# Attention block with feed-forward: weight sums, weight mixing, a copy and two norm stages moved in the hand-written order

## Chip, cores and metric

The kernel runs on one core of a Trainium2 chip. The metric is the device time of one execution in microseconds; the time of a kernel is the median of its runs. In the listings PE is TensorE, PEld its weight load, DVE VectorE, ACT ScalarE, POOL GpSimd and SP SyncE, which issues the DMAs. A letter L and a number name a line of the kernel.

## What is computed

One layer on 8 sequences of 1024 tokens, width 512, 16 heads of 32, inner width 2048, all fp32. Both sublayers are sandwiched between norms:

```
qvk = layernorm(x) @ Wqvk                      # q, v, k: 16 heads of 32
scores = einsum('bshi,bthi->bsth', q, k) + causal mask;  scores = scores / sqrt(512)
weights = softmax(scores, axis=2)
wv = einsum('bsth,bthi->bshi', weights, v)
x = x + layernorm(wv @ Wo)
hidden = layernorm(x) @ W1 + b1
imag   = w_imag * sin(theta + hidden * 0.1)
q      = hidden + (cos(theta) * w_real + sin(theta) * w_imag) * imag * 0.1
x = x + layernorm(relu(q) @ W2 + b2)
```

## The kernel before

**Batches and stages.** A loop runs over the 8 sequences, here called batches 0 to 7. For each, `attention` goes over four groups of four heads. Per group, `find_maxima` makes the scores in four runs and reduces each row to its maximum (matmuls L675; VectorE L693 and L705; exponentials and row sums for the first half, ACT L725). The maxima are split into three bf16 parts on GpSimd (L653, L660, L662) and transposed on TensorE (L114). Then `weigh` makes the scores again, transposed, with the maxima subtracted by a matmul (L781, L792), takes the exponentials (ACT L807) and masks the diagonal squares (GpSimd L811). `weighted_values` multiplies with v (L830) into an accumulator bank.

**Sums and division.** For the second half of the queries the weights of a group are added up on VectorE (`add_weights`, L859) and summed over keys by four-head matmuls with ones (`weight_sums`, L845). `divide` takes ACT Ln (L864) and Exp (L866) of the sum, and VectorE multiplies the accumulator (L867) into `wvT`. For the first half, the sums come into the exponentials through the maxima, and the accumulator is copied to `wvT` by ACT (L960). The last steps of a group are kept in `late` and `summing` and run inside the next group's `find_maxima`: after its first run, `sums()` is called.

**Fillers.** Between the runs of `find_maxima` generators fill TensorE: `advance(work, fill)` projects q, k and v of the next group (L513, L522, L530, with copies L538 on ACT and additions L565, L566 on GpSimd). The list `MAX_FILL` gives how many steps after each run. In the last group of batch 7 there is nothing left to project.

**After attention.** `finish_block` runs per half: projection (`project`, L1013), copy out (L1022), norm, addition to x, norm, transposition (L114) and mixing for the fast products (L1051). Half 0 runs inside attention's last group, half 1, `between`, inside the feed-forward.

**Feed-forward.** `feed_forward` has 8 steps of first-layer products and a ninth in which only second-layer products are left, numbered s = 0 to 8. Both layers use a scheme of seven products in place of eight. `hidden(s)` makes the first layer's products "1", "6", "2", "7", "5", "4", "3" (L1127) and combines them on VectorE (L1197) and ACT (L1210) into `hid`. `wave_in` (VectorE L1148, L1153, L1154, ACT sine L1155) and `wave_out` (VectorE L1170, L1176) apply the transform; `wave_out` of a step comes in the next one, but in step 7 in the same. `blocks` on GpSimd (L1243, four operations each) makes the mixed inputs hm of the second layer, whose products (L1262) follow in four quarters. A quarter is drained by ACT L1314 and VectorE L1274 into two tiles yb and then passes through `end`: bias on GpSimd (L1343), moments (VectorE L309, L310), rstd (GpSimd L316, L317), normalisation (L328), addition to x (L1352), store to HBM (L1356) and reload of x for the next batch (L121). `end` is a staged generator: stage by stage for the two tiles, advanced by `advance_ends(1)` in the loop of the feed-forward. `measure_ahead` takes moments of a later batch's input (xin, loaded at L391) in steps 7 and 8.

```
            (1, 2, 1, 3),
            (7,) * 6,
        )
        BETWEEN = ((0, 1, 2), (2, 3), (1, 3))
        MEASURE = {STEPS - 1: 2, STEPS: 7}
```

The first lines are the last two rows of `SECOND`: how many second-layer products follow each place of steps 7 and 8. `BETWEEN[s]` names the places of step s at which half 1 of `finish_block` goes on.

**Weights.** In batch 0 `mix_weights` prepares the mixed weights of both layers once: it loads parts (w_t), makes sums on GpSimd (L288) and stores all to scratch in HBM (L302). It is a generator of 34 pieces, advanced by `mixing` in the deferred steps of attention. Later, SP loads the mixed weights tile by tile (wm, L1103) into a ring of 18 buffers.

**Order.** Within each engine the order is that in which the kernel issues (`in_order`, `keep_in_program_order`); an engine takes its queue from the front. All eight PSUM banks of 2 KB per partition are given out in turn by `psum`, and `drained` marks the instruction after which a bank is free.

Of the kernel before, what the change touches and what calls it, by code (L numbers as in the profile page):

```python
# [32 lines left out]
def kernel(  # L33
# [14 lines left out]
    nc = tc.nc  # L48
# [61 lines left out]
    def in_order(instruction):  # L110
        tc.keep_in_program_order(instruction)
# [257 lines left out]
    def advance(work, steps=1):  # L369
        for _ in range(steps):  # L370
            if next(work, None) is None:
                return

    def finish(work):
        for _ in work:
            pass
# [120 lines left out]
    def project_qkv(b, g):  # L497
# [122 lines left out]
    MAX_RUNS = (  # L620
        (((0, 0), (2, 0)),),
        (((5, 0),), ((3, 0),)),
        (((4, 0),), ((1, 0), (5, 1))),
        (((6, 0),), ((4, 1), (6, 1))),
    )
# [10 lines left out]
    def find_maxima(b, g, work, sums, more):  # L636
# [84 lines left out]
        def exponentials(left):  # L721
            for es, cols, mx, row in left:
                for m in range(2):
                    in_order(
                        nc.scalar.activation(  # L725
                            es[:, m, cols],
                            es[:, m, cols],
                            AF.Exp,
                            bias=mx[:, m : m + 1],
                            scale=-1.0,  # L730
                            accum_out=row[:, m : m + 1],
                        )
                    )

        left = []
        for n, (run, fill) in enumerate(zip(MAX_RUNS, MAX_FILL[g > 0])):
            new = [x for pieces in run for x in run_unit(pieces)]
            if n == 0:
                sums()
            exponentials(left)  # L740
            left = new
            if n == len(MAX_RUNS) - 1:
                split(0)
            advance(work, fill)
            if n >= len(MAX_RUNS) - 2:
                advance(more)
        mT = transpose_maxima(parts_q[0], nc.scalar.copy)
# [10 lines left out]
    def transpose_maxima(parts, evacuate):  # L758
        pt = psum([P, TPB, P], BF16)
        for n in range(TPB):  # L760
            transpose_on_pe(pt[:, n, :], parts[:, n, :], ident_h)
        mT = small.tile([P, HALF], BF16, tag="mT", name="mT", bufs=2)
        evacuate(mT, pt.rearrange("p n t -> p (n t)"))
        drained(pt)
        return mT
# [104 lines left out]
    def attention(b, wvT, after):  # L870

        late = []
        adding = []
        summing = [None]

        def sums():
            if summing[0] is not None:
                summing[0]()  # L880
                summing[0] = None

        def flush():
            while late:
                late.pop(0)()

        def projections(g):
            if g + 1 < NG:
                return project_qkv(b, g + 1)
            if g + 1 == NG and b + 1 < B:  # L890
                return project_qkv(b + 1, 0)
            return iter(())

        work = projections(0)
        for g in range(NG):
            more, first = after(g)
            early = more if first is None else iter(())
            mT, later = find_maxima(b, g, work, sums, early)
            if not b and g + 2 < NG:
                mix_weights_of_group(b, g + 2)  # L900
            mTs = [mT]
            at = 0
            for c in range(2):
                accs = []
                total = None
                units = KEY_UNITS[c]
                for u, keys in enumerate(units):
                    if at < 2:
                        later(at)
                    weights, placed = weigh(b, g, c, keys, mTs[c])  # L910
                    if at < 2:
                        advance(work)
                    if at == 2:
                        mTs.append(
                            transpose_maxima(
                                parts_q[1], lambda *a: in_order(nc.vector.tensor_copy(*a))
                            )
                        )
                    if c and u == 0:
                        finish(work)  # L920
                        work = projections(g + 1)
                        advance(work)
                    if c and u == len(units) - 2:
                        advance(work)
                    if first is None and (at < 2 or c and u >= len(units) - 2):
                        advance(more)
                    while len(late) > (g < NG - 1 and c and u > 0):
                        late.pop(0)()
                    while adding and (g == NG - 1 or not late or u > 1):
                        add_weights(*adding.pop(0))  # L930
                    apart = g == NG - 1 and u >= len(units) - 2
                    if c and u == 0:
                        total = weights, placed
                    elif c and not apart:
                        adding.append((total[0], weights, placed))

                    def step(accs=accs, u=u, last=u == len(units) - 1, weights=weights, c=c, g=g,
                             placed=placed, total=total, apart=c and apart, dst=wvT[c][:, g, :]):
                        if u == 0:
                            accs.append(psum([P, HALF]))  # L940
                        acc = accs[0]
                        weighted_values(acc, b, g, u == 0, last, weights, placed)
                        if apart:
                            if not last:
                                accs.append(psum([P, HALF]))
                                weight_sums(accs[1], *total, last=False)
                            weight_sums(accs[1], weights, placed, first=False, last=last)
                        if last and c:

                            def whole():  # L950
                                if apart:
                                    whole_sum = accs[1]
                                else:
                                    whole_sum = psum([P, HALF])
                                    weight_sums(whole_sum, *total)
                                divide(acc, whole_sum, dst)

                            summing[0] = whole
                        elif last:
                            nc.scalar.copy(dst, acc)  # L960
                            drained(acc)

                    late.append(step)
                    advance(mixing)
                    if first is not None and at >= first:
                        advance(more)
                    at += 1
            while adding:
                add_weights(*adding.pop(0))
            if g == NG - 1:  # L970
                flush()
                advance(more)
                sums()
            else:
                finish(more)

                def ended():
                    flush()
                    sums()

                summing[0] = ended
        return more

    def finish_block(b, half, wvT, x2T, mixed, out_w):
# [75 lines left out]
    def feed_forward(b, x2T, mixed, before, between):  # L1060
# [3 lines left out]
        STEPS = 2 * NSTEP  # L1064
# [10 lines left out]
            (1, 2, 1, 3),  # L1075
            (7,) * 6,
        )
        BETWEEN = ((0, 1, 2), (2, 3), (1, 3))
        MEASURE = {STEPS - 1: 2, STEPS: 7}
        hids = {}  # L1080
        ahead = []
# [280 lines left out]
        def advance_ends(steps):  # L1362
            for _ in range(steps):
                while quarters and next(quarters[0], None) is None:
                    quarters.pop(0)
# [8 lines left out]
        for s, quota in enumerate(SECOND):  # L1374
            if s == NSTEP:
                finish(between)
            products = hidden(s) if s < STEPS else iter(())
            for n, more in enumerate(quota):
                advance(products)
                if s in MEASURE and n >= len(quota) - MEASURE[s]:  # L1380
                    advance(measuring)
                if s < len(BETWEEN) and n in BETWEEN[s]:
                    advance(between)
                advance_ends(1)
                if (s, n) == (1, 1):
                    advance(units)
                advance(units, more)
                if s == STEPS and n == 3 and b + 1 < B:
                    fetch(b + 1, 1)
                if s == STEPS and n >= 2:  # L1390
                    advance(mixing_x)
# [6 lines left out]
    mixing = mix_weights()  # L1398
# [81 lines left out]
```

## Time and profile before

| | |
|---|---|
| time, median of 3 runs | 3686.82 us (3686.36 to 3687.15) |
| profiled execution | 3686.16 us |
| its span | 3684.4 us |
| mean granted TensorE clock | 0.995 |
| TensorE busy | 3587.1 us, 97% |
| VectorE busy | 2752.1 us, 75% |
| ACT busy | 1453.6 us, 39% |
| GpSimd busy | 1451.3 us, 39% |
| moved by DMA | 488.83 MB, mean 133 GB/s |

The profile is one execution. A group's busy time is the sum over its instructions; a wait is idle time of an engine ahead of an instruction, put down to the instruction that released it last. Times inside the span count from the first instruction. Batch 4 is used as the example of a steady batch: its maxima for group 3 begin near 2039 us, its feed-forward's step 7 near 2268 us.

### The profile page before, as it was taken

How to read it: one execution, taken by the hardware profiler on the slowest of the kernel's cores; microseconds unless marked ns; L12 is line 12 of the kernel's file. 1: busy time of each engine (PE TensorE's matmuls, PEld its weight loads, DVE VectorE, ACT ScalarE, POOL GpSimd, SP SyncE). 2: the span in 40 equal slices, each digit the busy share in tenths (PEclk: the TensorE clock that was granted, in tenths of full speed). 3: DMA queues.
4: the chain of work that ended last, by engine and by line, in shares of the span. 5: the costliest groups of instructions: out<-in, count | busy, mean ns of one | idle time of the engine just before them, and what ended most of it. 6: DMA issues, size and time to landing. Idle time of an engine off the chain costs nothing.

```text
span 3684.4 us, 61975 instructions
## 1 busy us (share of the span) xinstructions
PE 3587.1 (97%) x22561; PEld 2342.0 (64%) x22561; DVE 2752.1 (75%) x5587; ACT 1453.6 (39%) x2812; POOL 1451.3 (39%) x1984
## 2 busy tenths in 40 slices
PE   8899999999999999999999999999999999999998
PEld 4446874478644786447864488544885548854587
DVE  5867777677686787767867778776887768777686
ACT  4553126531365213652146521465115642156310
POOL 5543363233532345313453234542344323543243
PEclk9999999999999999999999999999999999999999
DMA  4433761047610475105751058410683116820166
GB/s 145 150 134 118 240 212 44 30 128 241 206 41 21 144 245 186 53 10 161 252 162 53 12 177 264 131 53 15 195 275 105 47 35 197 263 78 18 58 216 190
DMA packets 312001, 488.83 MB, mean 133 GB/s; under 512 B 29904, under 2 KB 91408, under 8 KB 311696
## 3 DMA queue, kind: packets, MB, share of 16 engines
q1 hardware_dynamic: 309536, 483.02, 41.5%
q8 instruction: 180, 2.95, 0.3%
q10 hardware_dynamic: 2160, 1.84, 0.2%
q14 instruction: 125, 1.02, 0.1%
HBM read 451.71 MB, written 33.03 MB: 132 GB/s over the span
## 4 chain that ended last, share of the span: by engine, by line
PE 78%; DVE 12%; issue 5%; ACT 2%; POOL 2%; DMA 0%; SPq 0%; DVEq 0%; POOLq 0%; ACTq 0%
PE banks L1127 16%; PE banks L1262 16%; PE banks L545 8%; PE banks L675 8%; PE banks L530 6%; PE banks L1013 6%; PE banks L830 5%; PE banks L792 5%; PE banks L513 3%; DVE w L859 3%; PE banks L114 2%; PE banks L781 2%; DVE u L1148 1%; PE banks L845 1%; DVE u L1154 1%
## 5 line engine op out<-in xcount | busy, mean ns | idle before, releaser
L807 ACT ACTIVATE w<-banks 128x1024 f32<-128x1024 f32 (+1 forms) x640 | 562.1, 938 | 286.0 <-PE banks L792 285.4
L859 DVE TENSOR_TENSOR w<-w 128x1024 f32<-128x1024 f32 (+3 forms) x416 | 427.2, 1080 | 136.3 <-PE banks L830 130.4
L811 POOL TENSOR_SCALAR_AFFINE_SELECT w<-w 128x256 f32<-128x256 f32 x512 | 293.2, 592 | 547.9 <-ACT w L807 482.7
L1127 PE MATMUL banks<-x2T,wm 128*128 128x256 f32 x2048 | 477.3, 381 | 22.9 <-DVE hid L1197 15.8
L705 DVE CUSTOM_DVE_ANT_0 es<-banks,mask 128x128 f32<-128x128 f32 (+3 forms) x1024 | 432.2, 484 | 62.4 <-PE banks L675 62.4
L1262 PE MATMUL banks<-wm,hm 128*128 128x256 f32 x2048 | 472.9, 381 | 2.4 <-POOL hm L1243 1.8
L1127 PEld LDWEIGHTS banks<-x2T,wm 128*128 128x128 f32 x2048 | 387.2, 190 | 86.0 <-DVE hid L1197 19.0
L1155 ACT ACTIVATE u<-u 128x1024 f32<-128x1024 f32 x128 | 135.4, 1058 | 774.6 <-DVE u L1154 765.7
L1262 PEld LDWEIGHTS banks<-wm,hm 128*128 128x128 f32 x2048 | 388.4, 191 | 60.2 <-POOL hm L1243 8.1
L693 DVE TENSOR_REDUCE mx<-banks 128x1 f32<-128x512 f32 (+1 forms) x384 | 309.6, 861 | 122.7 <-PE banks L675 122.5
L1262 PE MATMUL banks<-wm,hid 128*128 128x256 f32 x1536 | 359.8, 380 | 6.5 <-DVE yb L1274 6.5
L1243 POOL TENSOR_TENSOR hm<-hid 128x256 f32<-128x256 f32 x256 | 216.6, 846 | 367.4 <-DVE hid L1176 367.4
L675 PE MATMUL banks<-k,q 32*128 32x512 f32 (+3 forms) x3072 | 329.6, 515 | 0.4 <-DVE mx L705 0.2
L792 PE MATMUL banks<-q,k 32*128 32x512 f32 (+3 forms) x3072 | 324.3, 492 | 0.0
L1262 PEld LDWEIGHTS banks<-wm,hid 128*128 128x128 f32 x1536 | 289.9, 190 | 48.2 <-DVE yb L1274 9.7
L830 PE MATMUL banks<-w,v 128*32 128x512 f32 (+3 forms) x3072 | 312.4, 495 | 5.4 <-POOL w L811 3.3
L530 PEld LDWEIGHTS banks<-wqvk,xnT 128*128 128x128 f32 x2048 | 242.0, 193 | 73.6 <-issue 50.9
L725 ACT ACTIVATE es<-es,mx 128x512 f32<-128x512 f32 (+3 forms) x512 | 279.6, 550 | 1.9 <-DVE mx L705 1.9
L530 PE MATMUL banks<-wqvk,xnT 128*128 128x128 f32 x2048 | 268.6, 283 | 0.0
L675 PEld LDWEIGHTS banks<-k,q 32*128 32x128 f32 x3072 | 154.0, 185 | 146.6 <-DVE mx L705 66.9
L1127 PE MATMUL banks<-mix,wm 128*128 128x256 f32 x1024 | 241.9, 379 | 0.0
L1013 PE MATMUL banks<-wo,wvT 128*128 128x512 f32 x512 | 235.6, 600 | 3.2 <-DVE wvT L867 3.2
(135 smaller groups left out, 5115.0 us busy)
## 6 DMA issues: line engine op xcount, KB each, us to landing
wm<-w_mixed SPq DMA_DIRECT2D x1344, 256.0 KB, 2.9
xin<-in_L_attn_h_dram SPq DMA_DIRECT2D x112, 256.0 KB, 4.0
wqvk<-in_L_attn_Wqvk_dram SPq DMA_DIRECT2D x93, 256.0 KB, 5.6
out_dram<-x SPq DMA_DIRECT2D x64, 256.0 KB, 2.0
x<-in_L_attn_h_dram SPq DMA_DIRECT2D x60, 256.0 KB, 3.2
w_mixed<-w_t SPq DMA_DIRECT2D x56, 256.0 KB, 3.0
wmix<-qk_mixed SPq DMA_DIRECT2D x42, 256.0 KB, 5.0
wo<-in_L_attn_Wo_dram SPq DMA_DIRECT2D x32, 256.0 KB, 2.7
```

The costliest lines, as they stand in the source:

```text
L530: nc.tensor.matmul(pv[:, t - t0, :], xnT[b, t // TPB][:, kc, (t % TPB) * P : (t % TPB + 1) * P], w_of[b, g, 1][:, kc, :], start=(kc == 0), ...
L545: nc.tensor.matmul(pq, w[:, kc0 + kc, :], moving[:, kc, :], start=kc == 0, stop=kc == 1,)
L675: nc.tensor.matmul(scs[j // 2][:, j % 2, at : at + n], queries[r, i * P : (i + 1) * P], keys[r, k0 : k0 + n], start=True, stop=True,)
L693: nc.vector.tensor_reduce(out=mx[:, m], in_=sc[:, m, cols], op=ALU.min, axis=mybir.AxisListType.X,)
L705: nc.vector.tensor_tensor_reduce(out=es[:, m, cols], in0=sc[:, m, cols], in1=mask[:, HALF - n :], scale=1.0, scalar=FMAX, op0=ALU.add, op1 ...
L792: nc.tensor.matmul(sts[j // 2][:, j % 2, cols], all_keys[r, kb * P : (kb + 1) * P], all_queries[r, q0 : q0 + n], start=False, stop=True,)
L807: in_order(nc.scalar.activation(w[:, :, :width], st[:, :, :width], AF.Exp, scale=-1.0))
L830: nc.tensor.matmul(acc[r, HALF - n :], v[b, g][:, kb, r], weights[j // 2][:, j % 2, cols], start=first and k == 0, stop=last and k == len( ...
L859: in_order(nc.vector.tensor_add(t[:, :, q], t[:, :, q], w[:, :, cols]))
L1013: nc.tensor.matmul(y, wvT[:, kc, t * P : (t + 1) * P], out_w[kc], start=(kc == 0), stop=(kc == KC - 1),)
L1127: nc.tensor.matmul(bank[:, n, :], w[:, n, kc, :], moving[:, kc, :], start=first and kc == 0 and n == 0, stop=kc == 1 and n == 1, skip_grou ...
L1262: nc.tensor.matmul(region, a[:, n], w[:, n], start=start and n == 0, stop=last and n == 1, skip_group_check=True,)
```

## The change

In `find_maxima` a second call of `sums()` stands behind the first filler, and `advance(mixing, 3)` behind the fillers of the first three runs; the advance of `mixing` in `attention`'s deferred step is gone. `sums()` now clears `summing` before it calls what was stored, and what is stored between groups is `flush` alone: the first call runs the last deferred step, which stores the sums, and the second call runs those. So the ones matmuls and the division come after the filler. The copy of the first half's accumulator goes from ACT to VectorE. In the feed-forward, the third place at which half 1 of `finish_block` goes on in step 0 is 3 in place of 2, and in step 7 `advance_ends` is called only at the last place.

```diff
@@ find_maxima
             advance(work, fill)
+            if n == 0:
+                sums()
+            if n < len(MAX_RUNS) - 1:
+                advance(mixing, 3)
             if n >= len(MAX_RUNS) - 2:
                 advance(more)
@@ attention
         def sums():
             if summing[0] is not None:
-                summing[0]()
-                summing[0] = None
+                summed, summing[0] = summing[0], None
+                summed()
...
                         elif last:
-                            nc.scalar.copy(dst, acc)
+                            in_order(nc.vector.tensor_copy(dst, acc))
                             drained(acc)
 
                     late.append(step)
-                    advance(mixing)
...
                 finish(more)
-
-                def ended():
-                    flush()
-                    sums()
-
-                summing[0] = ended
+                summing[0] = flush
@@ feed_forward
-        BETWEEN = ((0, 1, 2), (2, 3), (1, 3))
+        BETWEEN = ((0, 1, 3), (2, 3), (1, 3))
...
                 if s < len(BETWEEN) and n in BETWEEN[s]:
                     advance(between)
-                advance_ends(1)
+                if s != STEPS - 1 or n == len(quota) - 1:
+                    advance_ends(1)
```

The instructions stay the same in number and size; the copies alone change their engine. On TensorE, 23 sets of ones matmuls come after the 16 filler matmuls of L530 instead of before them, and in each batch one projection (L1013) comes after the products "5" and "4" of step 0. In the changed kernel line numbers are 4 higher from `find_maxima` into `attention`, and 2 lower from `finish_block` on.

## Prediction

> **What bounds the kernel now.** I read the page's busy times first, then TensorE's waits, then the timelines around the places that the diff touches. The profiled execution took 3686.16 us, its span 3684.4 us, so 1.76 us lie around the span; the median of the three runs is 3686.82, 0.66 more.
>
> ```profile
> PE 3587.1 (97%) x22561; PEld 2342.0 (64%) x22561; DVE 2752.1 (75%) x5587; ACT 1453.6 (39%) x2812; POOL 1451.3 (39%) x1984
> ...
> PE 78%; DVE 12%; issue 5%; ACT 2%; POOL 2%; DMA 0%; SPq 0%; DVEq 0%; POOLq 0%; ACTq 0%
> ```
>
> TensorE is the bound. The change adds and removes no matmul, so it can only open or close gaps of TensorE. This is the list of them (waiting matmul and line, what it waited for, total us, times, longest):
>
> ```profile
> PE banks L1127 <- DVE hid L1197: 15.8, 8, 2.0
> PE banks L781 <- ACT w L807: 13.7, 33, 0.5
> ...
> PE banks L845 <- DVE w L859: 11.2, 4, 4.7
> PE banks L1127 <- DVE u L1197: 7.1, 8, 0.9
> ...
> PE banks L830 <- POOL w L811: 3.3, 5, 1.0
> ...
> PE banks L1262 <- POOL hm L1243: 1.8, 6, 0.3
> ```
>
> The line of 15.8 us is one gap of 1.96 us per batch, in feed-forward step 7; the 11.2 us lie in batch 0.
>
> **1. Ends held back in step 7 (8 batches).** The gain first. In batch 4 VectorE does this in step 7 (start, duration):
>
> ```profile
> 2281.61 0.94 DVE L328 TENSOR_SCALAR yb<-yb,mv,rs 128x512 f32<-128x512 f32 x1
> 2282.58 1.09 DVE L1352 TENSOR_TENSOR x<-x,yb 128x512 f32<-128x512 f32 x1
> 2283.60 0.68 DVE L1197 TENSOR_TENSOR hid<-banks,u 128x512 f32<-128x512 f32 x1
> ```
> ```profile
> 2281.35 1.03 PE L1262 MATMUL banks<-wm,hm 128*128 128x256 f32 x4
> 2284.34 0.70 PE L1127 MATMUL banks<-x2T,wm 128*128 128x256 f32 x2 [1.96 <-DVE hid L1197]
> ```
>
> Two normalisations (L328), two additions (L1352) and one moment (L309, L310) of the finished quarter stand ahead of the hidden addition that product "3" waits for. Taken away, that addition ends by about 2281.5, TensorE goes on at 2282.38, and 1.96 us are gained.
>
> The price is on GpSimd. The second tile's rstd (L316, L317) is issued with these stages, and GpSimd works in order. Before:
>
> ```profile
> 2277.67 0.22 POOL L316 TENSOR_SCALAR rs<-mv 128x1 f32<-128x1 f32 x1 [3.43 <-DVE mv L310]
> 2277.97 0.57 POOL L317 TENSOR_TENSOR rs<-rs,mhalf 128x1 f32<-128x1 f32 x1
> ...
> 2282.23 0.90 POOL L1243 TENSOR_TENSOR hm<-hid 128x256 f32<-128x256 f32 x1
> 2283.21 1.05 POOL L1243 TENSOR_TENSOR hm<-hm,hid 128x256 f32<-128x256 f32 x1
> ...
> 2296.26 0.73 POOL L1243 TENSOR_TENSOR hm<-hid 128x256 f32<-128x256 f32 x1 [10.62 <-DVE hid L1176]
> ```
>
> There are three blocks of four hm operations behind the first rstd: at 2278.51, 2282.23 and 2296.26. In the changed order the rstd moves behind the block of 2278.51 and still stands ahead of the block of 2282.23. Its input, the second tile's moment, moves on VectorE to behind both wave_out of step 7. So the block of 2282.23, whose inputs are ready early, now waits behind the rstd for a moment that comes some 15 us later. Who waits for that block? The second-layer products with hm at 2291.35:
>
> ```profile
> 2291.35 1.03 PE L1262 MATMUL banks<-wm,hm 128*128 128x256 f32 x4
> ```
>
> They now have 2291.35 - 2283.21 - 1.05 = 7.1 us of slack. When does the moment end after the change? The first hidden addition starts when its product is done, 2280.8, the second when the product with mixl ends, 2281.4, and ends at 2282.1. From there VectorE's own row: first wave 2.8 (the same four operations take that at 2289.01 to 2291.88), addition 0.6, second wave 2.9, i.e. to 2288.4; the two wave_out took 2291.80 to 2296.11, 4.3, so to 2292.7. Then, in the changed order, one xin moment (0.8), the first tile's L328 (0.54 without a neighbour on GpSimd), L1352 (0.69) and the second tile's moment (0.9): 2295.6. The rstd takes 0.85, and the first two hm operations 1.55 (0.73 each in the 2296.26 rows, with a gap of 0.08): 2298.05. TensorE, 1.96 us earlier than before, arrives at 2289.4 and stands for 8.7 us. Against before the products start 2298.05 - 2291.35 = 6.7 us late. The gap of 0.29 at the third hm block goes, as that block follows by 2301.5 and is wanted at 2304. Net +6.4 per batch. Batches 6 and 7 have no xin moment there: +5.6. Sum 6 x 6.4 + 2 x 5.6 = **+49.6 us** (44 to 62: the hidden additions 0.7 us sooner, or both waves at the slower durations that they have beside GpSimd).
>
> SyncE: the two stores and the reload of x also move behind that point, so some ten wm loads queue behind a store that waits for L1352 until about 2298.5. A weight is used 15 us after its load may be issued and lands in 2.9 us at the median, and TensorE itself is 6.7 us late: hidden; without that cover I would count 2 to 3 us a batch. The drains of this quarter (L1274) come up to 2 us late, but the next quarter uses the other banks, and nobody wants these for 12 us.
>
> **2. Sums behind the first filler (23 places).** The ones matmuls (L845), ACT's Ln and Exp (L864, L866) and VectorE's product (L867) now come after 16 filler matmuls (L530), 1.98 us later. The second run of the maxima needs the banks that they free. In batch 4, group 3: L845 goes from 2040.05 to 2042.03, so Ln starts at 2043.32 and L867 ends after 0.60 + 0.63 + 0.68 plus 0.1 of handing over, at 2045.35. The matmuls that take its bank stood at 2044.17: +1.2 us, seven times, as batch 7 has no filler there. In groups 1 and 2 the ones matmuls now wait inside for the last addition L859, 0.94 us that the filler would hide; L867 then ends 1.2 after the moment when the bank is wanted: net +0.3, sixteen times. Sum 8.4 + 4.8 = **+13 us**. Bounds: the 0.92 gained sixteen times with no bank late, -15; 1.2 at all 23, +28. I take the middle, because the trace already shows the next run's weight loads (L675) waiting for L867, 4.8 us in 21 places.
>
> **3. Mixing of weights in the maxima (batch 0).** Before, GpSimd's additions (L288) run among the weights' exponentials:
>
> ```profile
> L288 POOL TENSOR_TENSOR w_t<-w_t x32: 1255/1308/2258, 74.6 to 265.3; 128x512 f32<-128x512 f32 x32
> ```
>
> Minimum, median and maximum are 1255, 1308 and 2258 ns: beside VectorE's L859 they stretch, and so do L859 and the masks L811. The weigh phases of groups 0, 1, 2 take 32.9, 30.6 and 32.3 us in batch 0 against 23.6, 23.6 and 24.3 in batch 4: 9.3 + 7.0 + 8.0, with a transposition gap of 1.54 some 25.9 us lost. The measuring of batch 1 stays in group 1 and keeps about 3.5 of that: 22.4 come back. In the new place the additions stand in GpSimd's queue ahead of the parts of the maxima (L653, L660) that the transpositions (L114) wait for: seven to eight additions of 1.27 in place of an idle GpSimd make those late by 4, 2.4 and 3.7 us, 9 us together. Net **-13 us** (between -26, when the delay is hidden, and +10, when each addition waits for its load besides).
>
> The stretching has a rule in the Trainium skill (GPSIMD Engine Reference, Specifications): GpSimd's SBUF interfaces are shared with VectorE and contended by VectorE instructions with two SBUF inputs. By it alone the maxima, which read PSUM, would return all 25.9, and the sum would be 13 us lower; it says nothing on the queue.
>
> **4. Copy to VectorE (32 copies).** L960 takes 616 ns on ACT; the nearest VectorE row is L867, 680 ns from PSUM. VectorE idles there for some 6 us before L859, which waits for TensorE anyway, and ACT's next exponentials wait for TensorE's scores: **0**. Bounds: -13.7 if all waits for L807 went, +22 (32 x 0.68) if all lay on the path. I take 0, since the 0.5 us gaps lie at ACT's own chain of four exponentials of 0.94.
>
> Against this edit speaks the skill's page Advanced Engine Details and Errata, The Read-Write Bubble, which puts ScalarE closer to PSUM and VectorE closer to SBUF. By the two rows that is 0.06 us a copy, 2 us in all if none were hidden.
>
> **5. One projection later (BETWEEN).** The gap of 0.89 (L1127 <- u) is VectorE's backlog in step 0; its work there stays the same: **0** (-7 to +7). The moved norm also issues an rstd, but the hm block behind it waits for a later wave_out in either order.
>
> **Sum.** 49.6 + 13 - 13 = +50: 3684.4 + 50 + 1.76 = 3736.2 for the profiled execution, about **3737** for the median.
>
> **Rivals.**
> - *Faster:* the block of 2282.23 is not held, because the second tile's moment ends before 2289.4 less 2.4, that is by 2287. Then the gaps of 1.96 and 0.29 of part 1, 2.25 us, are won eight times: -18 + 13 - 13 gives 3669. Against it: the moment stands behind both wave_out on VectorE, and these alone ended at 2296.11. It decides for faster as soon as the stall is under 2 us. 0.06.
> - *Slower, but by half:* the hold is there, sums and mixing both go to their good ends (-15, -26) and the copy takes some of the L781 waits: 44 - 15 - 26 - 5 = -2 up to +25, 3685 to 3712. 0.12, of it 0.04 within the bound of no change.
> - *Much slower:* bank waits at all 23 places, mixing +10, ends 62: +100, 3787; anything above 3765 gets 0.08.
> - *Forecast,* 3712 to 3765: 0.74.
>
> **How the numbers follow.** A measurement of this kernel can tell 0.2% from no change, 7.4 us. The range 3706 to 3766 holds the forecast and the upper part of the second rival, and leaves 2 in 10 out. Faster 0.06, same 0.04, slower 0.90.
>
> **What would show it.** Right: a line "PE banks L1260 <- POOL hm L1241" of some 60 to 75 us in 8 places, longest 8 to 9, in place of the 15.8 of "hid L1195", and L316 with a long idle time ahead of it, ended by VectorE's mv; about +1 at L675 in run 2 of the maxima; L845 gone from batch 0, L114 <- parts_q up by 9. Wrong: no hm wait beyond 1 us, or a step 8 whose products start earlier than before.

## Result and the profile after

The changed kernel takes 3768.58 us (median of 4 runs, 3766.94 to 3769.23) against 3686.88 of before: 81.7 us or 2.2% slower, ratio 1.0221 with the interval 1.0203 to 1.0239. The profiled execution took 3768.28 us with a span of 3766.4. The forecast was 3737, range 3706 to 3766: the direction and the main wait are right, the size lies just outside.

The page of the changed kernel: busy times and the chain that ended last.

```profile
PE 3611.8 (96%) x22561; PEld 2360.5 (63%) x22561; DVE 2760.3 (73%) x5619; ACT 1440.3 (38%) x2780; POOL 1442.6 (38%) x1984
...
PE 81%; DVE 9%; ACT 4%; POOL 3%; issue 3%; DMA 1%; SPq 0%; POOLq 0%; DVEq 0%; ACTq 0%
```

TensorE has the same 22561 matmul records but is busy for 24.7 us more: besides new waits, some matmuls run slower. TensorE's waits:

```profile
PE banks L1260 <- POOL hm L1241: 70.8, 8, 9.1
...
PE banks L114 <- POOL parts_q L660: 11.0, 3, 5.0
PE banks L1125 <- DVE u L1195: 10.2, 8, 1.3
...
PE banks L849 <- DVE w L863: 6.5, 5, 3.2
```

And the wait of its weight loads (PEld) for the product that ends the division, 4.8 us in 21 places before:

```profile
PEld banks L675 <- DVE wvT L871: 20.5, 23, 1.0
```

The wait for hm is there as forecast (60 to 75 us, 8 places, longest 8 to 9), the 15.8 us for hid are gone. The forecast waits for the parts (L114) and for `wvT` are there too. The ones matmuls' wait for the last addition of weights (L849 in the changed kernel) was to be gone from batch 0 and is not: 5.8 of the 6.5 us lie there. GpSimd in batch 4, where it now stands (start, duration, in brackets the idle time ahead):

```profile
2322.74 0.73 POOL L1241 TENSOR_TENSOR hm<-hid,hm 128x256 f32<-128x256 f32 x1
2341.52 0.22 POOL L316 TENSOR_SCALAR rs<-mv 128x1 f32<-128x1 f32 x1 [18.05 <-DVE mv L310]
2341.82 0.57 POOL L317 TENSOR_TENSOR rs<-rs,mhalf 128x1 f32<-128x1 f32 x1
2342.36 0.72 POOL L1241 TENSOR_TENSOR hm<-hid 128x256 f32<-128x256 f32 x1
2343.16 0.78 POOL L1241 TENSOR_TENSOR hm<-hm,hid 128x256 f32<-128x256 f32 x1
```

GpSimd idles for 18.05 us in front of the rstd. The moment that it waits for is the last of this row of VectorE:

```profile
2337.75 0.88 DVE L1174 TENSOR_SCALAR hid<-hid,prm 128x512 f32<-128x512 f32 x2
...
2340.52 0.69 DVE L309 BATCH_NORM_STATS2 st<-yb 128x6 f32<-128x512 f32 x1
2341.25 0.18 DVE L310 BATCH_NORM_AGGREGATE mv<-st 128x2 f32<-128x6 f32 x1
```

And TensorE starts 0.06 us after the second hm operation:

```profile
2333.71 1.24 PE L1260 MATMUL banks<-wm,hid 128*128 128x256 f32 x5
2344.00 5.21 PE L1260 MATMUL banks<-wm,hm 128*128 128x256 f32 x16 [9.05 <-POOL hm L1241]
...
2351.64 3.62 PE L1260 MATMUL banks<-wm,hm 128*128 128x256 f32 x16
```

These 16 matmul records take 5.21 us; the later group of 16 of the same kind takes 3.62. The windows of the stall and behind it show why (each row: stretch and its length, busy us of PE, PEld, DVE, ACT, POOL, then granted clock, DMA share, GB/s):

```profile
2334.95:2340.20 5.25, 0.00 (x0) 0.00 (x0) 5.18 (x12) 0.59 (x1) 0.00 (x0) 1.00 0.43 141
2340.30:2344.00 3.70, 0.00 (x1) 0.00 (x1) 3.39 (x7) 0.00 (x0) 2.32 (x5) 0.50 0.78 218
2344.00:2347.00 3.00, 3.00 (x7) 2.47 (x8) 1.28 (x3) 0.00 (x0) 2.92 (x4) 0.50 0.45 167
2347.10:2352.00 4.90, 4.90 (x24) 4.33 (x23) 0.00 (x0) 0.00 (x0) 4.29 (x7) 1.00 0.80 229
```

The granted clock is full for the first 5.25 us of the stall, half (0.50) for the rest of it and for the first 3 us of matmuls behind it, and then full again. Matmuls start 427 ns apart at first and 216 ns later. Over the span the granted clock is 0.986, against 0.995.

By stages (from the first matmul of the maxima to the first of the feed-forward, and from there to the next batch), the 82 us of TensorE's last end lie so: feed-forward +68.8 over eight batches (211.6 to 212.7 before, 219.4 to 221.4 now), attention of batches 1 to 6 +1.7 to +2.0 each, of batch 0 +3.3, of batch 7 -0.9.

### The profile page after: what moved, and what is told of

The parts are those of the page before. It is cut to its first block, busy times and chain, and to the rows that moved or that the text cites. A ratio compares the mean times of both kernels' runs of the same rounds, so it can differ in the third digit from the quotient of the medians.

```text
span 3766.4 us, 61929 instructions
## 1 busy us (share of the span) xinstructions
PE 3611.8 (96%) x22561; PEld 2360.5 (63%) x22561; DVE 2760.3 (73%) x5619; ACT 1440.3 (38%) x2780; POOL 1442.6 (38%) x1984
## 4 chain that ended last, share of the span: by engine, by line
PE 81%; DVE 9%; ACT 4%; POOL 3%; issue 3%; DMA 1%; SPq 0%; POOLq 0%; DVEq 0%; ACTq 0%
PE banks L1260 17%; PE banks L1125 17%; PE banks L545 7%; PE banks L675 7%; PE banks L834 6%; PE banks L530 6%; PE banks L796 6%; PE banks L1011 5%; PE banks L513 3%; PE banks L785 2%; PE banks L114 2%; ACT w L811 1%; DVE u L1146 1%; DVE u L1152 1%; PE banks L849 1%
## 5 line engine op out<-in xcount | busy, mean ns | idle before, releaser
L1260 PE MATMUL banks<-wm,hm 128*128 128x256 f32 x2048 | 488.5, 390 | 71.5 <-POOL hm L1241 70.8
L1125 PE MATMUL banks<-x2T,wm 128*128 128x256 f32 x2048 | 474.9, 380 | 10.2 <-DVE u L1195 10.2
L1260 PEld LDWEIGHTS banks<-wm,hm 128*128 128x128 f32 x2048 | 399.0, 196 | 134.0 <-POOL hm L1241 77.9
L863 DVE TENSOR_TENSOR w<-w 128x1024 f32<-128x1024 f32 (+3 forms) x416 | 421.1, 1066 | 63.5 <-PE banks L834 54.9
L675 PE MATMUL banks<-k,q 32*128 32x512 f32 (+3 forms) x3072 | 359.5, 519 | 3.6 <-DVE wvT L871 3.1
L530 PEld LDWEIGHTS banks<-wqvk,xnT 128*128 128x128 f32 x2048 | 240.4, 192 | 71.2 <-issue 49.2
L675 PEld LDWEIGHTS banks<-k,q 32*128 32x128 f32 x3072 | 166.8, 186 | 184.5 <-DVE mx L705 86.6
L530 PE MATMUL banks<-wqvk,xnT 128*128 128x128 f32 x2048 | 266.9, 282 | 0.0
```

Source lines behind the costliest of these rows:

```text
L530: nc.tensor.matmul(pv[:, t - t0, :], xnT[b, t // TPB][:, kc, (t % TPB) * P : (t % TPB + 1) * P], w_of[b, g, 1][:, kc, :], start=(kc == 0), ...
L675: nc.tensor.matmul(scs[j // 2][:, j % 2, at : at + n], queries[r, i * P : (i + 1) * P], keys[r, k0 : k0 + n], start=True, stop=True,)
L863: in_order(nc.vector.tensor_add(t[:, :, q], t[:, :, q], w[:, :, cols]))
L1125: nc.tensor.matmul(bank[:, n, :], w[:, n, kc, :], moving[:, kc, :], start=first and kc == 0 and n == 0, stop=kc == 1 and n == 1, skip_grou ...
L1260: nc.tensor.matmul(region, a[:, n], w[:, n], start=start and n == 0, stop=last and n == 1, skip_group_check=True,)
```

## Experiments

e1 to e5 each take one edit alone onto the kernel before. Differences are to the kernel before as measured beside each run (medians of 3686.64 to 3687.31 us); in brackets stand the ratio and its 95% interval.

### Ends held back in step 7 (e1_ends)

```diff
-                advance_ends(1)
+                if s != STEPS - 1 or n == len(quota) - 1:
+                    advance_ends(1)
```

> The kernel before with the one edit that holds the ends back in step 7. Theory (a rstd on GpSimd that waits for a moment holds the hm block behind it, and TensorE, having stood for 9 us, starts again at a lower clock): eight waits of L1260 for hm of about 9 us, seven to eight slow matmuls behind each, together 9.05 - 1.96 - 0.29 + 1.6 = 8.4 us a batch, 3754 us. Rival (the stall as the prediction has it, without the clock; the rest of the excess comes from the other edits): 6.4 to 6.8 us a batch, 3738 to 3741. Second rival (the stall needs the other edits too): no hm wait over 1 us, 3669.

Measured: 3753.48 us against 3687.31, +66.2 (ratio 1.0176, 1.0161 to 1.0191). TensorE waits:

```profile
PE banks L1262 <- POOL hm L1243: 70.8, 8, 9.0
```

The edit alone makes the whole hm wait. Waits add 70.8 - 15.8 - 1.8 = 53.2 us. Outside the waits, the starts of the feed-forward's matmuls exceed 216 ns by 26.5 us in all, against 13.2 in the kernel before: 13.3 more. Together 66.5: the eight feed-forwards grow by 66.8 in the two profiles, and the medians differ by 66.2. Behind each stall 9 to 13 matmul records are slow. The rival without the clock is 13 us short, the one that needs other edits falls.

### Weight sums behind the first filler (e2_sums)

```diff
             advance(work, fill)
+            if n == 0:
+                sums()
...
-                def ended():
-                    flush()
-                    sums()
-                summing[0] = ended
+                summing[0] = flush
```

> The kernel before with the sums alone behind the first filler. Theory (the banks come late by 0.2 to 0.3 us in groups 1 and 2 and by 1.2 to 1.3 in group 3): 16 x 0.25 + 7 x 1.25 = 13 us, 3700. Rival (the banks are no bound, only the wait for the last L859 is hidden): 3672.

Measured: 3692.25, +4.9 (1.0012, 1.0002 to 1.0021): neither number. Batches 1 to 6 cost 1.77 us each, as the theory says (0.2, 0.2 and 1.2 for the maxima of groups 1, 2 and 3 in batch 4). But batch 0 wins 4.4 us and batch 7 0.3.

```profile
PE banks L847 <- DVE w L861: 5.1, 4, 2.7
```

This wait, 11.2 us in all before (10.5 in batch 0), is that of the ones matmuls for the last addition of weights, which in batch 0 comes late; the filler hides 6 us of it. No stretch of batch 0 runs at half clock any more (10.2 us before), so a part of what it wins is the clock. 6 x 1.8 - 4.4 - 0.3 = 5.9.

### Mixing of weights in the maxima (e3_mixing)

```diff
             advance(work, fill)
+            if n < len(MAX_RUNS) - 1:
+                advance(mixing, 3)
...
                     late.append(step)
-                    advance(mixing)
```

> The kernel before with the mixing of weights alone moved into the maxima. Theory (GpSimd's additions and their waits for DMA stand ahead of the maxima's parts, and what the weigh phases win is lost at the transpositions): 3687, within 4 us. Rival, the prediction's term (13 us won, the delay being smaller than the gain): 3674.

Measured: 3691.08, +3.8 (1.0009, 1.0000 to 1.0019). The theory is nearer than the 13 us of gain. The waits that matter:

```profile
PE banks L847 <- DVE w L861: 11.5, 5, 5.2
PE banks L114 <- POOL parts_q L660: 9.6, 3, 4.1
```

The transpositions lose 9.6, near the prediction's 9, but the wait for the additions of weights has not gone: 11.5 against 11.2 before. GpSimd and VectorE in group 0 of batch 0 show the reason; the second view holds groups of operations (busy us, mean ns of one) between 94.5 and 98.7 us, while GpSimd's three additions run:

```profile
93.70 6.13 POOL L288 TENSOR_TENSOR w_t<-w_t 128x512 f32<-128x512 f32 x3
```
```profile
L861 DVE TENSOR_TENSOR w<-w 128x1024 f32<-128x1024 f32 x2 | 3.6, 1856 | 0.0
L861 DVE TENSOR_TENSOR w<-w 128x512 f32<-128x512 f32 x2 | 3.4, 1756 | 0.0
```

The additions are issued behind the first filler, but GpSimd has only masks left ahead of them and starts them at 93.70, before the maxima's first matmul at 95.6. So they still meet the end of VectorE's additions of weights. In batch 0 TensorE now stands at half clock for 20.5 us, against 10.2 before: a part of the loss is the restart behind these waits.

### Mixing later in the maxima (e10_mixing_later)

```diff
-            if n < len(MAX_RUNS) - 1:
-                advance(mixing, 3)
+            if n in (1, 2):
+                advance(mixing, 5)
```

> As e3_mixing, but the mixing goes on only behind the second and third run of the maxima, five pieces each, instead of behind the first three. Theory (behind the first run GpSimd starts the additions while VectorE still adds up weights, so the wait of L847 for these stays; behind the second run it has ended): the wait of L847 for L861 falls from 10.8 us to under 3, the wait of L114 for parts stays near 10 or grows by a few us: 3681 to 3688 against 3691 for e3. Rival (the wait of L847 has nothing to do with the mixing): it stays at 10 us, 3691 or more.

Measured: 3704.50, +17.7 (1.0049, 1.0032 to 1.0065), outside the theory's 3681 to 3688. Same group, same engine, now between 97.8 and 103.9 us, with no addition of GpSimd beside them:

```profile
L861 DVE TENSOR_TENSOR w<-w 128x1024 f32<-128x1024 f32 x4 | 4.9, 1265 | 0.0
L861 DVE TENSOR_TENSOR w<-w 128x512 f32<-128x512 f32 x2 | 1.3, 679 | 0.0
```
```profile
PE banks L114 <- POOL parts_q L660: 29.6, 3, 12.2
...
PE banks L847 <- DVE w L861: 6.1, 3, 3.1
```

Half of the theory holds: without the mixing beside it the 512-wide addition takes 679 ns in place of 1756, and the wait in group 0 is gone, so the rival falls although the time is on its side. (In groups 1 and 2 waits of 2.3 and 3.1 us remain; what causes them there was not tried.) The other half was much too low: the parts now make TensorE wait for 29.6 us in all, 12.2 at the longest, where GpSimd itself idles for 4.2 and 1.3 us ahead of its last two additions, the longer time for a load. TensorE is at half clock for 41 us of batch 0. Either place loses; the kernel before, which spread the additions among the masks, is the best of the three.

### One projection later (e4_between)

```diff
-        BETWEEN = ((0, 1, 2), (2, 3), (1, 3))
+        BETWEEN = ((0, 1, 3), (2, 3), (1, 3))
```

> The kernel before with the later place of one projection alone. Theory (the wait of L1127 for u grows from 0.89 to 1.28 us in each batch): 3690. Rival, the prediction's term: 3687, the wait as before.

Measured: 3689.55, +2.2 (1.0005, 0.9996 to 1.0015), by itself no more than the measurement can tell, but the wait is in every batch:

```profile
PE banks L1127 <- DVE u L1197: 10.2, 8, 1.3
```

7.1 before: 3.1 us more, 0.39 in each batch, as the theory has it.

### Copy on VectorE (e5_copy)

```diff
-                            nc.scalar.copy(dst, acc)
+                            in_order(nc.vector.tensor_copy(dst, acc))
```

> The kernel before with the copy of the first half's accumulator alone moved to VectorE. Theory (it lies in idle time of VectorE): 3687, within 3 us. Rival (the copies delay the additions of weights behind them): up to 32 x 0.68 = 22 us, 3709.

Measured: 3686.52 against 3686.64 (1.0000, 0.9991 to 1.0009). No difference, as forecast.

### The change without the held ends (e6_after_ends_back)

```diff
-                if s != STEPS - 1 or n == len(quota) - 1:
-                    advance_ends(1)
+                advance_ends(1)
```

> The changed kernel with the ends of step 7 put back as before. Theory (the held-back ends cost 66 us by themselves and the other edits add to them): no hm wait over 0.3 us, the hid wait of 1.96 us back in every batch, 3768.6 - 66 = 3702. Rival (the ends cost more in company): under 3695.

Measured: 3700.04, +13.4 over before (1.0035, 1.0021 to 1.0050). The gap for hid is back and no wait for hm is over 0.3 us:

```profile
PE banks L1125 <- DVE hid L1195: 15.8, 8, 2.0
```

The other four edits cost 13.4 together, 4.9 + 3.8 + 2.2 - 0.1 = 10.8 one by one.

### Filling the stall (e8_warm)

```diff
+            def keep_warm(other):
+                spare = psum([P, 2, QUART])
+                for k in range(18):
+                    in_order(nc.tensor.matmul(spare[:, 0], other[:, 0], x2T[1][:, 0, :QUART], ...))
+                drained(spare)
...
+                            if (half, q, j, n) == (1, 0, 2, 3):
+                                keep_warm(a["1"])
                             product(bank[:, m], a[name], j == 0 and m == 0, last)
```

> The changed kernel with 18 spare matmuls (128x256, into a bank that nothing reads) ahead of the product that waits for hm, 7.8 us of TensorE work in a stall of 9 us. Their result isn't used. Theory (the matmuls behind the stall are slow because TensorE stood): the seven matmuls behind the wait run at 216 ns from start to start in place of 427, the granted clock over the span rises, and the kernel with more work takes less time: 3768.6 - 8 x 1.6 = 3756. Rival (the slow matmuls come from something else, such as the weights or hm arriving late): 3768 or more.

Measured: 3751.89, that is 16.7 us less than the changed kernel (3768.58) for 63.5 us more of matmuls. The timeline of one stall:

```profile
2325.82 7.93 PE L1275 MATMUL banks<-x2T,hid 128*128 128x256 f32 x36
2335.03 4.00 PE L1260 MATMUL banks<-wm,hm 128*128 128x256 f32 x16 [1.28 <-POOL hm L1241]
```

The matmuls with hm still wait for the same late operation of GpSimd, but the 16 matmul records behind it take 4.00 us in place of 5.21, a feed-forward falls to 218 to 218.8 us, and the span's clock is 0.995 as before. So the slow matmuls come from TensorE having stood, and not from late data. In the changed kernel 7 to 13 slow records follow each stall.

### Holding only what does not feed GpSimd (e7_one_hold, e9_moments_first)

```diff
-                advance_ends(1)
+                if s != STEPS - 1 or n in (0, 3):
+                    advance_ends(1)
```

> The kernel before, in which step 7 lets the ends go on at its first and last place and holds them at the two between: the first tile's normalisation and the second tile's moment and rstd stay early, only the second tile's L328 and L1352 move behind both wave_out. Theory (the harm came from the rstd that waits, the gain from VectorE's two operations ahead of the hidden addition): the hid wait of 1.96 us goes or shrinks to 0.3 at most, no hm wait, 8 x 1.7 to 2.2 us won, 3669 to 3673. Rival (VectorE's backlog comes out elsewhere, at the drains or hm): 3687.

Measured: 3677.45, -9.2 (0.9973, 0.9962 to 0.9984). The wait for hid is gone and nothing is held on GpSimd's queue, but a new wait of 1.2 us a batch takes half of the gain:

```profile
PE banks L1262 <- POOL hm L1243: 9.3, 8, 1.4
```

It is the third hm block, whose hid VectorE has not finished. The next kernel has the same hold and takes the first tile's two operations out of that chain too, by a new order of the ends' stages, in all quarters (lines joined here):

```diff
-            return staged(len(ybs), measure, add, store)
+            def stages():
+                measure(0); yield True
+                measure(1); yield True
+                add(0); yield True
+                store(0); add(1); yield True
+                store(1); yield True
+            return stages()
```

> As e7_one_hold, but the ends take both tiles' moments (and rstd) before the first tile's L328 and L1352, so that these too are held until both wave_out of step 7 are issued. Theory (e7's remaining hm wait of 1.2 us a batch is VectorE's chain of step 7, of which L328 and L1352 of the first tile are 1.2 us): the hm wait goes, 8 x 1 us less than e7, 3669 to 3671. Rival (the hm wait is GpSimd's or the held operations delay the drains): as e7, 3677.

Measured: 3668.07, -18.7 (0.9948, 0.9933 to 0.9963), with 5.3 us of hm waits left. By stages 15.6 us of it lie in the feed-forwards; 1.4 us are won behind the last matmul, where the new order also acts.

### Best version (e11_best)

The kernel of e9_moments_first, and in `find_maxima` (the other lines of e2_sums come with it):

```diff
             if n == 0:
                 sums()
+                if b:
+                    sums()
...
             advance(work, fill)
+            if n == 0:
+                sums()
```

> e9_moments_first with the sums behind the first filler in batch 0 alone, where e2_sums won 4.4 us, and as before in all other batches, where it lost 1.8 each. Theory: 4 us less than e9_moments_first, 3665. Rival (the start's DMA waits take it back): as e9_moments_first.

Measured: 3664.51, -22.3 (0.9939, 0.9924 to 0.9954), the fastest here: the gap that the change aimed at in step 7 is closed without the hold on GpSimd, and the sums are late only where the filler hides a wait.

## Why the prediction was right in direction and short in size

**Ends in step 7: the mechanism right, a term missing.** The step from the changed order to GpSimd's hold stood word for word in the trace: 18 us of idle GpSimd ahead of the rstd, a stall of 9.05 us forecast as 8.7, 8.26 in the batches without xin moment (0.8 less, as forecast), no line of SyncE among the waits. The waits net to 53.2 us where the sum said 49.6. The step that failed here is the conversion of a stall into time: "TensorE, 1.96 us earlier than before, arrives at 2289.4 and stands for 8.7 us" was charged at 8.7, as though matmuls ran at full rate at once. The restart costs 13.3 us over the eight stalls (e1, e8). The signs of it were in the profile before (columns as above): TensorE was at half clock for 3.4 us behind a wait of 2.9 us for L859 in batch 0, and likewise behind the very gap of 1.96 us that the edit was to close, in batches 1 and 3, whose feed-forwards take 212.7 us in place of 211.6.

```profile
101.40:104.70 3.30, 3.30 (x11) 1.64 (x12) 2.74 (x17) 1.23 (x2) 0.00 (x0) 0.50 0.93 304
927.50:930.70 3.20, 3.20 (x9) 2.49 (x9) 3.02 (x5) 0.72 (x1) 0.00 (x0) 0.50 0.99 350
```

In e7, e9 and e11, where that gap is closed, no feed-forward has a stretch at half clock.

The Trainium skill has the rule (TensorE: Matmul & The Clock Gate, What's actually happening): after an idle window of about 3.4 us TensorE's clock halves, until it has been busy for about as long again. The stall in batch 4 agrees: full clock for 5.25 us, then half, and full again 3 us behind the restart. The gaps of 1.96 us do not: they are shorter than the page's window, and two of the eight were followed by half clock all the same. There the measurement decides.

**Sums: the steady term right, batch 0 missed.** Forecast +0.3, +0.3 and +1.2 for groups 1, 2 and 3, measured 0.2, 0.2 and 1.2. What was left out is that batch 0's ones matmuls already waited 10.5 us for the additions of weights (of the line's 11.2, which the prediction puts there whole), and the filler hides more than half: 13 forecast, 4.9 measured.

**Mixing: the term with the wrong sign.** Forecast -13, measured +3.8: 16.8 us apart, as large a miss as the ends' 16.6. The wait that speaks against the edit was nearly right (9 us at the transpositions, 9.6 measured; 11.0 in the full change), though it too costs a restart. The step that failed is "22.4 come back", read from lengths of phases: measured the same way, from the first matmul of a group's second half (L781, L783 in e3) to the second run of the next maxima, the three phases take 27.7, 25.9 and 33.1 us in e3 against the prediction's 32.9, 30.6 and 32.3, and 9.1 come back. Inside these phases lie the 10.5 us of waits of the ones matmuls, and those stayed: 10.8 us in e3's batch 0. Up to the next maxima's first matmul group 0 did get shorter, 19.4 to 16.7 us, but not the wait behind it, because moving an instruction in the issue order moves it in time only if its engine is busy up to there. GpSimd had only masks left to do and started the additions beside the same additions of VectorE. e3 and e10 together show it for group 0; in groups 1 and 2 the rest of the wait is not explained.

**Copy:** 0 forecast, -0.1 measured. **BETWEEN:** 0 forecast, +2.2 measured, with 3.1 us more wait for u. The argument that VectorE's work there stays the same was not enough: the wait grew by 0.39 us a batch; which of the moved operations makes it was not singled out.

**The sum:** 66.2 + 4.9 + 3.8 + 2.2 - 0.1 = 77.0 against 81.7. The rest of 4.7 lies within the intervals of the single runs, each of some 3 to 6 us to either side. The stages put it into batch 0's attention: +3.3 us in the changed kernel and +2.5 in e6, where e2 and e3 alone give -4.4 + 2.8 = -1.6. There TensorE is at half clock for 17.1 us in the changed kernel, 0 in e2 and 20.5 in e3: what the late sums win there is mostly lost beside the moved mixing. Why is open; no run separates the two.

Against the forecast of +50, the ends are 16.6 us too low, the mixing 16.8, BETWEEN 2.2 and the rest 4.7, the sums 8.1 too high. Without the restart, or with the mixing's term right, the result would have been inside the range; that it lies only 2.6 us outside is partly luck, as the sums made up for a half of one miss.

## What to carry to other kernels

When an instruction that waits is moved, look at every queue that its stage issues into: here one pair of operations of 0.8 us on GpSimd per batch, moved with VectorE's work, cost more than all else, and keeping the moments early while holding only the additions turned a loss of 66 us into a gain of 19. Price a stall of TensorE with its restart: here 1.5 to 2.9 us behind 8 to 9 us, and 1.1 us behind two of eight gaps of 1.96. And an operation given to an idle engine runs when its inputs are there, not where it stands in the text; to keep two engines apart, something ahead must hold the queue.

## What the runs showed of the hardware

In the changed kernel stalls of 8.26 to 9.05 us were followed by 7 to 13 slow matmul records (427 ns from start to start, two records per 128x256 fp32 product), 1.5 to 2.9 us each time at the same place, so the restart is no fixed price: the clock was half for 6.8 us around three of the stalls (7 or 8 slow records) and for 10.2 us around the other five (11 to 13). And 18 spare products per batch in the stall made the same kernel 16.7 us faster. VectorE's 512-wide addition of two SBUF tiles takes 679 ns alone (e10) and 1756 beside GpSimd's additions (e3), which stretch from 1.26 to between 1.6 and 2.2 us at the same time: both lose.
